# Layer 1 of a four-layer image network: column hats placed by 0/1 matmuls in three groups of rows, and PSUM in single banks

## The chip, the core and the metric

The kernel runs on one NeuronCore of a Trainium2 chip. The metric is device time in microseconds for one execution, and the time given is the median of several runs. All arithmetic is fp32.

## The reference

The input `x` has 8 images of 384 channels and 32 x 32 pixels. Four layers follow each other, each as `x = x + layer(group_norm(x))`: layer 0 is attention over the pixels, layer 1 a deformable convolution, layer 2 attention over the channels, layer 3 a sum of depthwise convolutions. The change lies in layer 1, whose core is this:

```
c3, c5, c7 = split(x, 3, axis=1)                    # 128 channels each, K = 3, 5, 7
for each c, K:
    offsets = conv2d(c, ow, ob, pad=K//2)           # 2*K*K planes: dy, dx of every tap
    acc = 0
    for each tap k = (ky, kx):
        py = y - pad + ky + dy_k;  px = x - pad + kx + dx_k
        acc += bilinear(c, py, px) * w[c, k]        # zero outside of the image
    out = conv1x1(acc, pw, pb)
out = concat(out3, out5, out7)
out = out * sigmoid(fc2(relu(fc1(mean(out)))) + fc2(relu(fc1(max(out)))))
```

A bilinear sample weighs a pixel by a product of two hats, `relu(1 - |py - row|)` and `relu(1 - |px - column|)`. So a sample is a sum over the pixels of a patch, weighted by a row hat times a column hat.

## The kernel before, in words

Layers 0, 2 and 3 stand before and after layer 1 and are, but for one statement in layer 0, not touched. Layer 1 (`layer1`) runs over 8 images and, for each, over the three kernel sizes ("cells", `CELLS`: r = 0, 1, 2 for K = 3, 5, 7).

**Cells, strips, tasks.** The output positions are cut into cells of `th x tw` pixels; all samples of a cell lie in a patch of `wy x wx` pixels: 8 x 16 = 128 for K = 3 and 5, 12 x 10 = 120 for K = 7. A strip is a column of cells (K = 3, 5: four strips, nine pixels wide) or three columns (K = 7: seven strips, six wide, the last with only two taps across). A task is one strip with a group of tap rows: ky 0 to 2 for K = 3; 0 to 2 and 3 to 4 for K = 5; 0 to 3 and 4 to 6 for K = 7. An image has 4 + 8 + 14 = 26 tasks.

**What one task needs.** 
- The patch's pixels, transposed so that pixels lie on partitions: `xw`, loaded by `patches` from DRAM images (L631), four transfers on GpSimd's queue for each column of cells.
- The sample weights: a tile of `weights` (two of them, in turn), pixel on the partition and (tap, position) along the row. `sample_weights` loads the row hats into it (`s<-hat`, L655: four transfers, each row hat repeated over the columns), loads the column hats of two tap rows each into a `plane` (`pl<-hat`, also L655, four transfers each, two buffers, each column hat repeated over the rows), and multiplies the one by the other on VectorE, one instruction for each tap row (L675).
- `sample` then multiplies the patches by the weights on TensorE (L704), two patches into a pair of PSUM banks, two such pairs in turn, and ScalarE copies a pair to SBUF (L712, tile `z`).
- `accumulate` adds `z` times the tap's weight to the accumulator on VectorE (L738), one instruction for each tap.

**Where the hats come from.** `offsets` normalizes the image (L213), transposes it and writes the DRAM images (`im<-xT`, L510), convolves the offsets on TensorE (L530; weights `cw` loaded on SyncE's queue, L523, for up to four taps, two buffers), adds positions and writes them to DRAM (`pos<-off`, L551). `hats` reads them back (`d<-pos`, L569, on SyncE's queue), makes hats on ScalarE (L583, L594) and writes them to DRAM (`hat<-hs`, L611, on ScalarE's queue).

**Order.** Layer 1 is under a manual schedule: every engine's instructions stand in the order in which the program emits them. The main loop goes over tasks. In turn i it issues the loads of task i + 1 (row and column hats) and part of the next strip's patches. Then it goes over slots, two patches each: one slot of task i's samples, a share of task i - 1's accumulations, and steps of the two background stages `offsets` and `hats`, which are paced by `LEADS` (0.75 and 0.6 of an image ahead) in equal steps per slot. If `hats` comes to a unit whose offsets aren't finished, `advance` runs the rest of those offsets at once. After the slots come the products (L675) of task i + 1. `end` projects a finished K (TensorE, L221 by the helper `project`), and after the third K the gate, as a "tail", is spread over the next slots (`or<-od` loads, L791; L792).

In layer 0, `zeros` is set and `clear` writes zeros to the DRAM images and to parts of the hats (L161, L170, GpSimd's queue) before the first image is loaded.

Of the kernel before, what the change touches and what calls it, by code (L numbers as in the profile page):

```python
# [40 lines left out]
class Cells:  # L41
# [8 lines left out]
    def __init__(self, ks, th, tw, nc, up, down, left, right, groups):  # L50
# [18 lines left out]
        if self.wx == 16:  # L69
            self.blocks = [(0, 0, 0, 0), (64, 8, 0, 0), (32, 0, 4, 0), (96, 8, 4, 0)]  # L70
            self.rows, self.lines = self.wy, list(range(self.wx))
        else:
            self.blocks = [(0, 0, 0, 0), (64, 0, 4, 0), (32, 0, 8, 0), (96, 8, 0, 4)]

            self.rows, self.lines = 32, [0, 1, 2, 3, 4, 5, 6, 7, 8, 8, 8, 9, 9, 9, 9, 9]
# [23 lines left out]
PLANE = 2 * max(c.ks * c.sp for c in CELLS)  # L99
# [25 lines left out]
def kernel(ctx: ExitStack, tc: tile.TileContext, t, out):  # L125
# [21 lines left out]
    for r, g in enumerate(CELLS):  # L147
        for i in range(2):
            images[r, i] = dpool.tile([g.cols, g.wy, g.ny, P], F32, tag=f"im{r}{i}", name=f"im{r}{i}")
            for a, n in enumerate((g.rows, len(g.lines))):  # L150
# [119 lines left out]
    def layer0():  # L270
        with tc.tile_pool(name="l0w", bufs=1) as wp, tc.tile_pool(name="l0", bufs=1) as sp, tc.tile_pool(
# [17 lines left out]
            nc.vector.memset(zeros, 0.0)  # L289
            clear(zeros)  # L290
# [114 lines left out]
            for i in range(len(todo) + 1):  # L405
                ahead = todo[i] if i < len(todo) else None
# [28 lines left out]
    def layer1(x2):  # L435
        with tc.tile_pool(name="l1w", bufs=1) as wp, tc.tile_pool(name="l1", bufs=2) as sp, tc.tile_pool(
            name="l1v", bufs=1, space=PSUM
        ) as pv, tc.tile_pool(name="l1m", bufs=2, space=PSUM) as pm, tc.manual_schedule():
# [22 lines left out]
            for i in range(2):  # L461
                h = wp.tile([P, max(g.pitch for g in CELLS) * H], F32, tag=f"hs{i}", name=f"hs{i}")
                nc.vector.memset(h, 0.0)
                hs.append(h)
            weights, sums = [], []
            for i in range(2):
# [3 lines left out]
                v = pv.tile([P, 2, HALF], F32, tag=f"v{i}", name=f"v{i}")  # L470
                nc.vector.memset(v, 0.0)
                sums.append(v)
            state = {}
            turn = [0]

            def offsets(b, r):
# [13 lines left out]
                for n0 in range(0, -(-N // px), QCH):  # L490
                    chunks = range(n0, min(n0 + QCH, -(-N // px)))
                    pt = pm.tile([P, QCH, P], F32, tag="m", name=f"pt_{b}_{r}_{n0}")
# [3 lines left out]
                    xT = sp.tile([P, QCH, P], F32, tag="tmp", name=f"xT_{b}_{r}_{n0}")  # L496
# [18 lines left out]
                po = pm.tile([P, N], F32, tag="m", name=f"po1_{b}_{r}")  # L515
                for ky in range(ks):
                    for kx in range(ks):
                        k = kx % WCH
                        if k == 0:
                            m = min(WCH, ks - kx)  # L520
                            cw = sp.tile([P, WCH * CELLS[-1].pm], F32, tag="cw", name=f"cw_{b}_{r}_{ky}_{kx}")
                            cw = cw[:, : m * g.pm].rearrange("p (k o) -> p k o", k=m)
                            nc.sync.dma_start(cw, t[f"ow{r}"][:, ky, kx : kx + m])  # L523
                        y, x = PAD - ks // 2 + ky, PAD - ks // 2 + kx
                        rows = H // g.pieces
                        for i in range(g.pieces):
                            for h in range(max(1, g.pn // HALF)):
                                n = min(g.pn, HALF) // W
                                y0 = y + i * rows + h * n
                                mm(  # L530
                                    po[i * g.pm : (i + 1) * g.pm, h * HALF : h * HALF + n * W],
                                    lhsT=cw[:, k, :],
                                    rhs=xp[:, y0 : y0 + n, x : x + W],
# [3 lines left out]
                        yield  # L537
                m = g.pieces * g.pm
                off = sp.tile([P, N], F32, tag="off", name=f"off_{b}_{r}", bufs=1)
                place = sp.tile([P, N], F32, tag="tmp", name=f"place_{b}_{r}")  # L540
                nc.sync.dma_start(place[:m, : g.pn], t[f"place{r}"])
                nc.scalar.activation(off[:m, : g.pn], po[:m, : g.pn], AF.Identity, bias=om[r])  # L542
# [11 lines left out]
            def hats(b, r):  # L554
# [9 lines left out]
                def load(kx, part):  # L564
                    d = sp.tile([P, N], F32, tag="d", name=f"d_{b}_{r}_{kx}_{part[0]}", bufs=1)
                    at = 0
                    for a in part:
                        w = (g.wy, len(g.lines))[a]
# [11 lines left out]
                for j, (kx, part) in enumerate(todo):  # L580
# [22 lines left out]
                    for a in part:  # L603
                        w = (g.wy, len(g.lines))[a]
# [35 lines left out]

            def sample_weights(i, b, r, s, k0, k1):

                g = CELLS[r]
                lo, nk = g.taps(s)
                tap = nk * g.sp
                wt = weights[i % 2]

                def spread(dst, a, ky, m):

                    tiles = hatsof[r, a, b % 2]  # L650
                    hat = tiles[0][s] if nk == g.ks else tiles[1][0]
                    src = hat[0, ky, 0, :]
                    row = g.ks * tap
                    for p0, x0, y0, more in g.blocks:
                        nc.gpsimd.dma_start(  # L655
                            dst[p0 : p0 + 32, : m * tap],
                            bass.AP(
                                tensor=src.tensor,
                                offset=src.offset + (x0 if a else y0) * row,
                                ap=[[row if a else more * row, 8], [0 if a else row, 4], [1, m * tap]],  # L660
                            ),
                        )

                pairs = [(ky, min(2, k1 + 1 - ky)) for ky in range(k0, k1 + 1, 2)]
                planes = []
                for ky, m in pairs:
                    pl = sp.tile([P, PLANE], F32, tag="plane", name=f"pl_{i}_{ky}")
                    spread(pl, 1, ky, m)
                    planes.append(pl)
                spread(wt[:, SGAP:], 0, k0, k1 + 1 - k0)  # L670
                yield
                for j, (ky, m) in enumerate(pairs):
                    for y in range(m):
                        dst = wt[: g.q, SGAP + (ky + y - k0) * tap :][:, :tap]
                        nc.vector.tensor_tensor(dst, dst, planes[j][: g.q, y * tap : (y + 1) * tap], ALU.mult)  # L675

            def sample(i, b, r, s, k0, k1):
# [10 lines left out]
                for p0 in range(i0, i1 + 1, 2):  # L688
                    n = min(2, i1 + 1 - p0)
                    v = sums[(p0 - i0) // 2 % 2]  # L690
                    for j in range(n):
                        y0 = (p0 + j) * g.th
                        lo, hi = max(k0, y0 - (H - 1)), min(k1, y0 + g.th - 1)
                        for x in range(s * g.nc, min((s + 1) * g.nc, g.nx)):
# [8 lines left out]
                            dst = v[:, j, : taps * g.th * g.sw].rearrange("p (k t x) -> p k t x", t=g.th, x=g.sw)  # L703
# [10 lines left out]
                        v[:, :n, : taps * g.th * g.sw].rearrange("p j (k f) -> p j k f", k=taps),  # L714
# [33 lines left out]
            def end(b, r):  # L748
                acc = state.pop(("acc", b, r)).rearrange("p h w -> p (h w)")
                po = pm.tile([P, N], F32, tag="m", name=f"pp_{b}_{r}")  # L750
                project(po, [pw[:, r, :]], [acc])
# [4 lines left out]
                nc.scalar.activation(o, po, AF.Identity, bias=pb[:, r : r + 1], accum_out=se[:, r, 0:1])  # L756
# [3 lines left out]
                yield  # L760
                nc.vector.tensor_reduce(se[:, r, 1:2], o, AX.X, ALU.max)
# [5 lines left out]
                pf = pm.tile([P, N], F32, tag="m", name=f"pf_{b}")  # L767
# [6 lines left out]
                for c in range(CT):  # L774
                    for i in range(2):
                        mm(
                            pf[:, HALF + c : HALF + c + 1],
# [7 lines left out]
                nc.scalar.activation(gate, pf[:, HALF : HALF + CT], AF.Sigmoid)  # L785
# [9 lines left out]
            def run(gen):  # L795
                for _ in gen:
                    pass
# [32 lines left out]
            def slots_of(b, r, s, k0, k1):  # L830
                return -(-((H - 1 + k1) // CELLS[r].th - k0 // CELLS[r].th + 1) // 2)
# [559 lines left out]
```

## Time and profile before

| | |
|---|---|
| median of 3 runs | 10046.43 us (10031.03 to 10050.84) |
| the profiled execution's own time | 10028.23 us |
| its span, first to last instruction | 10026.3 us |
| mean granted TensorE clock | 0.805 |
| TensorE busy | 6818.8 us (68%) |
| VectorE busy | 3773.1 us (38%) |
| ScalarE busy | 2332.4 us (23%) |
| GpSimd busy | 1798.7 us (18%) |
| moved by DMA | 1500.81 MB in 587308 packets |
| of that from GpSimd's queue (q0) | 1045.17 MB |

Every line of a group names the line of the kernel, the engine, the operation and the tiles as `out<-in`, then shape and count; in brackets is the idle time of the engine just before, with what ended it. Each fp32 matmul appears as two MATMUL and two LDWEIGHTS instructions. The busy share in forty slices has one digit for each 250 us. GpSimd's transfers show as busy time of that engine (issue); a transfer on SyncE or ScalarE as a row of SPq or ACTq.

### The profile page before, as it was taken

To read this page: it belongs to the slowest core of one execution; us is meant where nothing else is said; L and a number is where in the kernel's file an instruction comes from. 1 tells how busy PE (TensorE), PEld (TensorE's weight loads), DVE (VectorE), ACT (ScalarE), POOL (GpSimd) and SP (SyncE) were. 2 spreads that over 40 slices of the span, in tenths; PEclk is the share of its full clock that TensorE was granted. 3 is DMA by queue.
4 is the path that set the end of the run, shared out by engine and by line. 5 is a ranking of instruction groups with operands and counts; after the bars stand their busy time and mean duration, and the time that the engine had idled before them with its cause. 6 is when DMAs were issued, how large, how long until landed. Compare 5 with 4: busy or idle time off the path is not lost.

```text
span 10026.3 us, 90890 instructions
## 1 busy us (share of the span) xinstructions
PE 6818.8 (68%) x35337; PEld 4023.8 (40%) x35337; DVE 3773.1 (38%) x6046; ACT 2332.4 (23%) x3107; POOL 1798.7 (18%) x3352
## 2 busy tenths in 40 slices
PE   6899999999655556555645645645655554888854
PEld 2334444444223433443433433434334444444443
DVE  2233333333213434444444444344344455222232
ACT  1222222222213223232232132232232221111100
POOL 0000000000012322232233233233233332000001
PEclk8889999999876777767867867767777776888877
DMA  2130000000137857777688688688687686000053
GB/s 72 35 47 21 18 7 18 18 14 12 49 120 253 247 189 262 223 254 240 202 275 246 190 283 250 184 278 245 187 269 237 221 275 204 19 21 24 19 153 106
DMA packets 587308, 1500.81 MB, mean 150 GB/s; under 512 B 249124, under 2 KB 411180, under 8 KB 525972
## 3 DMA queue, kind: packets, MB, share of 16 engines
q0 software_dynamic: 291424, 1045.17, 33.4%
q1 hardware_dynamic: 154896, 312.55, 10.3%
q10 hardware_dynamic: 140548, 137.17, 4.5%
q8 instruction: 283, 4.64, 0.2%
q14 instruction: 157, 1.29, 0.0%
HBM read 1245.01 MB, written 248.48 MB: 149 GB/s over the span
## 4 chain that ended last, share of the span: by engine, by line
PE 46%; DMA 34%; DVE 6%; issue 4%; ACT 4%; POOL 3%; SPq 2%; ACTq 1%; DVEq 0%; POOLq 0%
PE po L530 9%; DMA xw<-im 8%; PE s L343 6%; DMA s<-hat 6%; PE pa L366 6%; PE s L355 5%; DMA pl<-hat 5%; PE v L704 4%; DMA cw<-in_ow_dram 3%; PE pqk L1087 3%; DVE s L675 3%; DMA hat<-hs 2%; PE po L221 2%; PE pc L1200 2%; POOL pl L655 2%
## 5 line engine op out<-in xcount | busy, mean ns | idle before, releaser
L704 PE MATMUL v<-s,xw 120*128 120x168 f32 (+6 forms) x10560 | 2108.1, 365 | 2012.3 <-DVE s L675 1048.5
L704 PEld LDWEIGHTS v<-s,xw 120*128 120x128 f32 (+1 forms) x10560 | 1881.5, 239 | 2363.1 <-issue 1696.6
L712 ACT ACTIVATE z<-v 128x1008 f32<-128x1008 f32 (+9 forms) x1536 | 988.8, 654 | 3223.9 <-PE v L704 2638.1
L738 DVE SCALAR_TENSOR_TENSOR acc<-z,dw,acc 128x192 f32<-128x192 f32 (+8 forms) x3496 | 1468.5, 425 | 669.5 <-ACT z L712 559.1
L675 DVE TENSOR_TENSOR s<-s,pl 120x1344 f32<-120x1344 f32 (+3 forms) x648 | 882.2, 1418 | 1414.8 <-DMA s<-hat 945.7
L530 PE MATMUL po<-xp,cw 128*98 128x512 f32 (+2 forms) x2944 | 1014.9, 617 | 525.5 <-DMA cw<-in_ow_dram 525.5
L655 POOL DMA_DIRECT2D pl<-hat x1408 | 752.1, 553 | 2443.7 <-DVE s L675 2263.9
L345 DVE TENSOR_REDUCE mx<-s 128x1 f32<-128x1024 f32 x512 | 604.5, 1219 | 1292.3 <-PE s L343 1292.2
L631 POOL DMA_DIRECT2D xw<-im x864 | 462.3, 547 | 2685.7 <-DMA im<-xT 1973.6
L358 ACT ACTIVATE e<-s 128x1024 f32<-128x1024 f32 x512 | 498.2, 1021 | 1480.6 <-PE s L355 1480.5
L530 PEld LDWEIGHTS po<-xp,cw 128*98 128x98 f32 (+2 forms) x2944 | 325.9, 156 | 1061.1 <-issue 891.4
L355 PE MATMUL s<-q,k 49*128 49x512 f32 x2048 | 651.4, 648 | 93.5 <-DVE mx L345 68.8
L343 PE MATMUL s<-k,q 49*128 49x512 f32 x2048 | 650.8, 669 | 5.4 <-ACT e L358 2.5
L366 PE MATMUL pa<-e,va 128*49 128x512 f32 x2048 | 615.5, 634 | 3.2 <-ACT e L358 3.2
L655 POOL DMA_DIRECT2D s<-hat x768 | 409.8, 547 | 703.8 <-PE v L704 481.2
L343 PEld LDWEIGHTS s<-k,q 49*128 49x128 f32 x2048 | 369.8, 316 | 277.3 <-issue 189.3
L355 PEld LDWEIGHTS s<-q,k 49*128 49x128 f32 x2048 | 267.4, 195 | 453.8 <-issue 263.7
L544 DVE TENSOR_REDUCE viol<-off 128x1 f32<-128x256 f32 (+2 forms) x24 | 18.6, 776 | 959.9 <-ACT off L542 959.9
L1200 PE MATMUL pc<-xT,hk 32*32 32x232 f32 (+6 forms) x9984 | 242.1, 436 | 174.1 <-issue 90.9
L1216 POOL DMA_DIRECT2D xr<-x x96 | 51.1, 550 | 1483.6 <-DVE gs L206 1082.2
L1087 PE MATMUL pqk<-wqk,xn 128*128 128x384 f32 x768 | 270.3, 517 | 9.5 <-DVE xn L213 9.5
L1200 PEld LDWEIGHTS pc<-xT,hk 32*32 32x32 f32 x9984 | 179.6, 114 | 236.2 <-issue 146.1
(141 smaller groups left out, 4309.4 us busy)
## 6 DMA issues: line engine op xcount, KB each, us to landing
pl<-hat POOLq DMA_DIRECT2D x576, 336.0 KB, 6.6
s<-hat POOLq DMA_DIRECT2D x192, 672.0 KB, 12.7
xw<-im POOLq DMA_DIRECT2D x608, 208.0 KB, 12.2
s<-hat POOLq DMA_DIRECT2D x192, 504.0 KB, 8.2
pl<-hat POOLq DMA_DIRECT2D x256, 360.0 KB, 6.5
s<-hat POOLq DMA_DIRECT2D x128, 540.0 KB, 8.9
s<-hat POOLq DMA_DIRECT2D x128, 360.0 KB, 7.6
hat<-hs ACTq DMA_DIRECT2D x112, 378.0 KB
```

What stands on the lines that cost most here:

```text
L343: mm(ps[j][:, hs], lhsT=q[rows, n:N:QCH], rhs=k[rows, hs], start=True, stop=True)
L345: nc.vector.tensor_reduce(mx[:, j, n : n + 1], ps[j], AX.X, ALU.max, negate=True)
L355: mm(ps[j][:, hs], lhsT=k[rows, n * P : (n + 1) * P], rhs=q[rows, hs], start=True, stop=True)
L366: mm(pa[rows, halves[h]], lhsT=va[:, n, 2 * g + j, :], rhs=state["e", n % 2, j][:, halves[h]], start=(n == 0), stop=(n == QCH - 1),)
L530: mm(po[i * g.pm : (i + 1) * g.pm, h * HALF : h * HALF + n * W], lhsT=cw[:, k, :], rhs=xp[:, y0 : y0 + n, x : x + W], start=(ky == 0 and k ...
L655: nc.gpsimd.dma_start(dst[p0 : p0 + 32, : m * tap], bass.AP(tensor=src.tensor, offset=src.offset + (x0 if a else y0) * row, ap=[[row if a ...
L675: nc.vector.tensor_tensor(dst, dst, planes[j][: g.q, y * tap : (y + 1) * tap], ALU.mult)
L704: mm(dst[:, (lo - k0) * nk : (hi + 1 - k0) * nk, :, xl * g.tw : (xl + 1) * g.tw], lhsT=state["xw", b, r, s][: g.q, xl, p0 + j, :], rhs=rhs ...
L712: nc.scalar.activation(z[:, :, yy : yy + n * g.th, :].rearrange("p k (j t) x -> p j k (t x)", j=n), v[:, :n, : taps * g.th * g.sw].rearran ...
L738: nc.vector.scalar_tensor_tensor(dst, z[:, (ky - k0) * nk + kx - first, ky - i0 * g.th : ky - i0 * g.th + H, bx : bx + x1_ + 1 - x0], dw[: ...
L1087: mm(pq[:, i, :C], lhsT=xn[:, c, n * P : (n + 1) * P], rhs=wqk[:, c, i * C : (i + 1) * C], start=(c == 0), stop=(c == CT - 1),)
L1200: mm(ps[32 * j : 32 * j + 32, i, lo * B : hi * B], lhsT=hk[32 * i : 32 * i + 32, j, (RL - d) * PITCH : (RL - d) * PITCH + W], rhs=xT[32 * ...
```

## The change

The column hats are no longer repeated by DMA. `load_columns` loads each of the patch's `wx` columns once, for two (K = 3, 5) or three (K = 7) tap rows at a time, into a tile `hx`: the row is cut into three parts (`PARTS`), which lie at partitions 0, 32 and 64. These loads are on SyncE's queue, three for each `hx`, five buffers, and stand two tasks ahead. For each tap row, three matmuls with a matrix of zeros and ones (`sel`) put the columns on the patch's pixels, each part into one of three PSUM banks (`columns`, one buffer), and VectorE multiplies the row hats by that PSUM tile. The products of task i + 1 stand in the second half of task i's slots.

PSUM is laid out anew: three single banks for the samples instead of two pairs, with as many patches in a bank as fit (`together`), one bank for transposes, projections and the gate, one for the offset convolution, three for `columns`. So the K = 7 convolution does one half of the image after the other, and loads its weights twice (four `cw` buffers); the projection does its halves one by one. The steps that pace the background are counted for the new loops. The hats of K = 7 are made for ten columns and not for sixteen lines. In layer 0 the clearing of the DRAM images stands at the fifth pair of heads of the main loop.

```diff
+        self.column = [0] * P
+        for p0, x0, _, more in self.blocks:
+            for p in range(32):
+                self.column[p0 + p] = x0 + (p // 12 if more else p // 4)
+        self.deep = 32 // self.wx
...
+PARTS = 3
+PART = max(c.ks * c.sp for c in CELLS) // PARTS
+SEL = [(w, m, j) for w in sorted({c.wx for c in CELLS}) for m in range(1, 32 // w + 1) for j in range(m)]
...
-            nc.vector.memset(zeros, 0.0)
-            clear(zeros)
...
             for i in range(len(todo) + 1):
+                if i == PAIRS:
+                    tc.keep_in_program_order(nc.vector.memset(zeros, 0.0))
+                    clear(zeros)
...
+            sel = wp.tile([P, len(SEL), P], F32, tag="sel", name="sel")
+            nc.scalar.dma_start(sel, t["sel"])
...
-                v = pv.tile([P, 2, HALF], F32, tag=f"v{i}", name=f"v{i}")
+            for i in range(3):
+                v = pv.tile([P, HALF], F32, tag=f"v{i}", name=f"v{i}")
...
+            columns = pv.tile([P, PARTS, HALF], F32, tag="columns", name="columns")
...
-                po = pm.tile([P, N], F32, tag="m", name=f"po1_{b}_{r}")
-                for ky in range(ks):
-                    for kx in range(ks):
...
+                for h in range(max(1, g.pn // HALF)):
+                    n = min(g.pn, HALF)
+                    po = pm.tile([P, HALF], F32, tag="c", name=f"po1_{b}_{r}_{h}")
+                    for ky in range(ks):
+                        for kx in range(ks):
...
-            def sample_weights(i, b, r, s, k0, k1):
+            def load_columns(i, b, r, s, k0, k1):
...
+                for ky in range(k0, k1 + 1, g.deep):
+                    m = min(g.deep, k1 + 1 - ky)
+                    hx = sp.tile([P, PART], F32, tag="hx", name=f"hx_{i}_{ky}", bufs=5)
                     src = hat[0, ky, 0, :]
-                    for p0, x0, y0, more in g.blocks:
-                        nc.gpsimd.dma_start(
-                            dst[p0 : p0 + 32, : m * tap],
...
+                    for c in range(PARTS):
+                        nc.sync.dma_start(
+                            hx[32 * c : 32 * c + m * g.wx, :n],
                             bass.AP(
...
+                                tensor=src.tensor, offset=src.offset + c * n, ap=[[g.ks * tap, g.wx], [tap, m], [1, n]]
                             ),
                         )
+                    state["columns", i] += [(hx, m, j) for j in range(m)]
...
-                for j, (ky, m) in enumerate(pairs):
-                    for y in range(m):
-                        dst = wt[: g.q, SGAP + (ky + y - k0) * tap :][:, :tap]
-                        nc.vector.tensor_tensor(dst, dst, planes[j][: g.q, y * tap : (y + 1) * tap], ALU.mult)
+                for ky, (hx, m, j) in enumerate(state.pop(("columns", i))):
+                    k = SEL.index((g.wx, m, j))
+                    for c in range(PARTS):
+                        rows = slice(32 * c, 32 * c + m * g.wx)
+                        mm(columns[: g.q, c, :n], lhsT=sel[rows, k, : g.q], rhs=hx[rows, :n], start=True, stop=True)
+                    dst = wt[: g.q, SGAP + ky * tap :][:, :tap].rearrange("p (c n) -> p c n", c=PARTS)
+                    nc.vector.tensor_tensor(dst, dst, columns[: g.q, :, :n], ALU.mult)
+                    yield
+
+            def together(r, s, k0, k1):
+                g = CELLS[r]
+                return HALF // ((k1 - k0 + 1) * g.taps(s)[1] * g.th * g.sw)
...
-                for p0 in range(i0, i1 + 1, 2):
-                    n = min(2, i1 + 1 - p0)
-                    v = sums[(p0 - i0) // 2 % 2]
+                few = together(r, s, k0, k1)
+                for p0 in range(i0, i1 + 1, few):
+                    n = min(few, i1 + 1 - p0)
+                    v = sums[turn[1] % len(sums)][:, : n * taps * g.th * g.sw].rearrange("p (j f) -> p j f", j=n)
+                    turn[1] += 1
...
-                po = pm.tile([P, N], F32, tag="m", name=f"pp_{b}_{r}")
-                project(po, [pw[:, r, :]], [acc])
...
+                for h in range(2):
+                    hs_ = slice(h * HALF, (h + 1) * HALF)
+                    po = pm.tile([P, HALF], F32, tag="m", name=f"pp_{b}_{r}_{h}")
+                    mm(po, lhsT=pw[:, r, :], rhs=acc[:, hs_], start=True, stop=True)
+                    nc.scalar.activation(o[:, hs_], po, AF.Identity, bias=pb[:, r : r + 1], accum_out=half[:, h : h + 1])
...
-                sum(g.ks**2 + 6 + -(-H // g.th // QCH) for g in CELLS),
+                sum(g.ks**2 * max(1, g.pn // HALF) + 6 + -(-H // g.th // 4) for g in CELLS),
...
                 if i + 1 < len(tasks):
-                    need(1, tasks[i + 1][:2])
                     nxt = sample_weights(i + 1, *tasks[i + 1])
                     next(nxt)
+                    n = tasks[i + 1][4] - tasks[i + 1][3] + 1
+                    products = [slots // 2 + (slots - slots // 2) * k // n for k in range(n)]
+                    if i + 2 < len(tasks):
+                        need(1, tasks[i + 2][:2])
+                        load_columns(i + 2, *tasks[i + 2])
...
-                        while nadd < total * (j + 1) / (slots - 1):
+                        while nadd < total * (j + 1) / slots:
...
+                    for _ in range(products.count(j)):
+                        next(nxt)
...
+    sel = np.zeros((P, len(SEL), P), np.float32)
+    for k, (wx, m, j) in enumerate(SEL):
+        column = next(c.column for c in CELLS if c.wx == wx)
+        for i in range(PARTS):
+            for x in range(wx):
+                sel[32 * i + x * m + j, k] = np.array(column) == x
```

## The prediction

> **What bounds the kernel now.** I read the page first: the span, then the 40 slices.
>
> ```profile
> span 10026.3 us, 90890 instructions
> ...
> PE   6899999999655556555645645645655554888854
> ...
> DVE  2233333333213434444444444344344455222232
> ...
> PEclk8889999999876777767867867767777776888877
> DMA  2130000000137857777688688688687686000053
> ```
>
> Three stages show. In the ends (layers 0, 2 and 3) TensorE is full and the DMA engines are idle. Between 2700 and 8500 us (layer 1, where the change lies) no engine is full: TensorE about 0.55, VectorE 0.4, DMA 0.75. So layer 1 is bound by waits, and I need them by region. One image takes 704 to 708 us there; the view of busy time by stretches, cut at one image's borders (3x3 cells; 5x5 cells; 7x7 cells; a block of offset convolution inside the 7x7 cells; their rest), gives:
>
> ```profile
> core 0: us, PE busy (x) PEld busy (x) DVE busy (x) ACT busy (x) POOL busy (x), PEclk, DMA share, GB/s
> 5092.00:5188.00 96.00, 35.44 (x159) 30.31 (x159) 34.25 (x54) 30.35 (x55) 34.14 (x64) 0.66 0.87 292
> 5188.00:5404.00 216.00, 128.56 (x531) 78.77 (x532) 89.78 (x135) 65.45 (x109) 63.76 (x120) 0.75 0.78 257
> 5404.00:5619.00 215.00, 109.37 (x619) 96.19 (x619) 119.86 (x220) 58.98 (x72) 76.60 (x144) 0.73 0.87 265
> 5619.00:5692.00 73.00, 73.00 (x168) 27.24 (x167) 0.00 (x0) 1.05 (x1) 0.00 (x0) 1.00 0.18 46
> 5692.00:5800.00 108.00, 50.37 (x295) 48.52 (x294) 66.19 (x136) 33.46 (x45) 42.24 (x80) 0.67 0.72 220
> ```
>
> TensorE works 397 of 708 us and VectorE 310; where the convolution does not run alone, DMA is near 0.9. The timeline of one 7x7 task shows why (columns: start, us, engine, line):
>
> ```profile
> 5462.94 4.27 POOL L655 DMA_DIRECT2D pl<-hat  x8 [12.03 <-DVE s L675]
> 5467.49 0.54 POOL L655 DMA_DIRECT2D s<-hat  x1 [0.28 <-PE v L704]
> ...
> 5470.98 1.04 POOL L655 DMA_DIRECT2D s<-hat  x2 [1.94 <-DMA pl<-hat]
> ...
> 5491.66 5.96 DVE L675 TENSOR_TENSOR s<-s,pl 120x1344 f32<-120x1344 f32 x4 [15.19 <-DMA xw<-im]
> ...
> 5496.26 1.19 PE L704 MATMUL v<-s,xw 120*128 120x126 f32 x4 [23.46 <-DVE s L675]
> ```
>
> The column hats (pl) can load only when VectorE has freed the planes, the row hats (s) queue behind them on GpSimd, the four products come 20 us later, and TensorE waits 23.5 us. A strip (two tasks) takes 55 us here (product at 5436.28, next at 5491.66). This wait for data, not an engine, sets layer 1; "DMA xw<-im" in the brackets is just the transfer seen last. The chain of waits over the image agrees, and names the other large piece, the convolution L530:
>
> ```profile
> by line: PE po L530 15.3%; DMA s<-hat 13.8%; DMA xw<-im 12.6%; DMA pl<-hat 7.9%; PE v L704 7.1%; DMA cw<-in_ow_dram 5.6%; issue 4.7%; DVE s L675 4.3%; DMA im<-xT 3.4%; POOL pl L655 3.3%; DMA or<-od 3.1%; DVE acc L738 1.7%; SPq L510 1.7%; DM
> ```
>
> **Two rules of the Trainium skill.** "TensorE: Matmul & The Clock Gate", Part 3 (Packing small matmuls), says that matmuls whose contraction fits 32 rows run at the same time when their operands start at different partitions 32i, and gives 3.07x for four. The nearest trace row has two groups of rows, at 0 and 64:
>
> ```profile
> 1002.06 2.11 PE L343 MATMUL s<-k,q 49*128 49x512 f32 x8
> ```
>
> Alone, an instruction of 512 columns takes 0.437 us (168 in 73.48 us, the block above), so eight would take 3.5: a gain of 1.66, not 2. It fits if each fp32 matmul is two instructions, the two of one matmul follow each other, and the next matmul starts with the second: five steps of 0.437 = 2.18. I go by the trace. "DMA: Bandwidth & Descriptors", section "Issuing engines are not separate DMA queues", says all queues share the same 16 engines, so moving loads from GpSimd to SyncE buys only issue time. The trace agrees as far as it goes (DMA share 0.75 over the image with three queues), so I count bytes, not queues.
>
> **Step 1, what leaves.** By the DMA issues of one image, pl is 192 transfers and 50.3 MB of 167.6. The new hx loads carry each row once, not 8 or 12 times: 20.0 MB / 8 + 30.3 MB / 12 = 5 MB. Left: 122 MB. GpSimd loses 192 x 0.55 = 106 us of issue; more to the point, s no longer stands behind 4.3 us of pl issue and 2.7 MB of pl data. At 290 GB/s (DMA nearly full above) s lands 9 us (2.0 MB) or 12 us (2.7 MB) after issue, 2 us of latency included; now it takes 20 to 28 from the first pl. SyncE gains 123 issues of about 0.35 us (43 us); it queues them ahead of its cw and d loads, but they are for two tasks on, with five buffers, so I cost them at nothing. If that cover fails, cw comes later still.
>
> **Step 2, what TensorE gains.** 81 products an image (12, 20, 42 and 7, of 3 x 288, 480, 448 and 128 columns). At 0.854 ns a column one pass is 0.25, 0.41, 0.38 and 0.11 us. By the pattern above three groups take 4 passes, plus 0.2 for changing the array's shape (the first L343 took 820 ns, the others 589): 1.2, 1.8, 1.7, 0.65 us, in all 14 + 36 + 71 + 5 = 126 us an image. Bounds: 2 passes, 56 us; in turn, 6 passes and the change of shape, 184 us.
>
> **Step 3, VectorE.** Same 648 products; one operand is now in PSUM. No such row exists; L395 (PSUM) takes 1283 ns and L792 (SBUF) 1285 for the same shape, so nothing is added. They no longer come as one burst at the task's end, but are spread over the second half, and TensorE waits for each before the next, since there is one `columns` buffer.
>
> **Step 4, the path by region**, TensorE's order with the waits that I expect.
> - 7x7 strip: samples 12.1 + 10.1, products 7 x 1.7 = 12, waiting for the last product at two task starts 2, for s in the second task 5 (products can start after seven slots, 8 us, and s needs 12): 41 us against 55. VectorE's 49 x 0.424 + 7 x 1.55 = 31.6 fits under it. Six strips 246; short strip 24 (now 30).
> - Convolution: its pace counts steps, and halving each 7x7 step makes 161 steps an image for 107. Counting the loop through, the block in the 7x7 cells falls from 42 steps x 4 instructions (73.5 us) to 64 x 2 (56 us); 30 steps (26 us) and 13 of 5x5 (8 us) are spread over the strips, 12 us of that inside waits for s; its cw loads stall about 13 x 1.5 = 20. 7x7 in all: 246 + 24 + 56 + 34 - 12 + 20 = 368, now 396.
> - 5x5: per strip samples 17, products 5 x 1.8 = 9, waits 6: 32 x 4 = 128; convolution 10, cw stalls 10, projection and hats on ScalarE 8: 156, now 216 (cw alone stalled it some 50).
> - 3x3: samples 4, products 3.6, waits 5: 12.6 x 4 = 50, and the tail's od/or transfers, unchanged, 26: 76, now 96.
>
> 600 us an image for 708. First and last image have other shares of convolution, so I count 7 images, not 8: -750 us. Single PSUM banks: 87 more evacuations an image x 0.155 us of fixed cost (from 1008 columns in 1.051 and 756 in 0.827) = 13 us of ScalarE, hidden under TensorE; the projection's second half waits for the first to be read, 24 x 1 = 24 us, within the 8 above. If ScalarE's hats hold up the three buffers, that cover is gone, at about 2 us each for 22 hats an image.
>
> **Step 5, layer 0.** The clearing of the images starts at pair 4, not at 10 us. It now delays kflat (20 us) and three or four divisions (den, inv, bc: 53, 41, 23, 20 us). Later it meets the same divisions of other pairs; only the start is won. I take -20, between -40 and +40.
>
> Sum against the profiled execution (10028.2 us, span 10026.3): 10028 - 750 - 20 = 9258. The profiled execution lies 18 us below the median of the three runs (10046.43): 9276, rounded **9280**.
>
> **Rivals.**
> - *Row groups in turn.* Step 2 at its upper bound: +58 an image. For it: L343's 1.66 instead of 2. 600 + 58 = 658, times 7: 9280 + 406 = about 9690.
> - *TensorE fits better.* Step 2 at 56 us and s early enough for no wait: 600 - 70 = 530, 9280 - 490 = 8790. For it: the clock, 0.75 now, rises with denser work (1.00 in the block).
> - *Turn-taking, slower.* One `columns` buffer, and both engines in order: each of 81 products keeps TensorE until VectorE has drained what is ahead, product 1.55 plus two slots' accumulations (4 x 0.42) = 3.2 us, 260 an image, of which I counted about 80. 780 an image, 7 x 72 = +500 on the time before: 10,550. It decides from 1.3 us a product (108 / 81) beyond mine. Against: VectorE is busy only 310 of 708.
> - *No change.* Row groups in turn and s as late as now (13 us landing plus issue, 2 to 5 more a task): about 10,030.
>
> **Numbers.** Forecast 0.52, in turn 0.18, better 0.13, slower 0.14, no change 0.03. A measurement of this kernel tells 0.2% from no change. Faster 0.83, same 0.03, slower 0.14. The range, 8650 to 9950, holds the first three with their bounds and leaves out 0.17.
>
> **What would show it.** Right: pl and its 50 MB gone, DMA share about 0.6; product matmuls in threes of about 1.5 us; six 7x7 strips near 41 us; convolution blocks of 128 instructions, 56 us; an image near 600. Wrong: product groups of 2.3 us (in turn); TensorE waiting on VectorE's product two or three us each time (turn-taking); s landing at 13 us or later; cw stalls grown because SyncE stands at an hx load.

## The result, and the profile after

The changed kernel takes 10,156.76 us (median of 6 runs, 10,141.92 to 10,180.61) beside 10,050.42 us for the kernel before in the same session: a ratio of 1.0104, interval 1.0082 to 1.0127. It is 1.0% slower. The forecast was 9,280.

The page of the profile after, the span and the slices (one digit for each 250 us):

```profile
span 10161.1 us, 99025 instructions
...
PE   8887999999755676676776766766766776788854
...
DMA  1113000000145555655565565566566565000053
```

What was to leave has left: in layer 1 the DMA share falls from 7 or 8 tenths to 5 or 6, and TensorE's digits rise from about 5 to 6 or 7. And yet nothing is won. Two marks in the traces say where the time is. They are the first patch load of layer 1 and the first matmul of layer 2, before and then after (duration in ns, minimum/median/maximum; first and last start in us):

```profile
L631 POOL DMA_DIRECT2D xw<-im x864: 508/546/737, 2708.1 to 8424.0; - x173
L1087 PE MATMUL pqk<-wqk,xn x768: 486/486/1008, 8522.3 to 9450.0; 128*128 128x384 f32 x192
```

```profile
L646 POOL DMA_DIRECT2D xw<-im x864: 506/567/987, 2782.3 to 8557.2; - x173
L1140 PE MATMUL pqk<-wqk,xn x768: 486/486/980, 8664.8 to 9587.6; 128*128 128x384 f32 x192
```

Layer 1 starts 74 us later, so layer 0 lost 74. It takes 5,882 us for 5,814 and loses 68. The rest gained 8.

One image of layer 1, busy time by stretches (3x3; 5x5; 7x7; the block of convolution inside the 7x7 cells). The border between 5x5 and 7x7 is the first 7x7 sample here; the prediction's lay some 28 us later, so I compare those two as a sum.

```profile
5199.00:5275.00 76.00, 46.59 (x230) 33.98 (x230) 34.19 (x53) 21.63 (x37) 17.98 (x35) 0.70 0.76 256
5275.00:5486.00 211.00, 127.70 (x551) 72.80 (x548) 86.78 (x131) 69.76 (x143) 28.74 (x56) 0.77 0.56 173
5486.00:5916.00 430.00, 310.76 (x1472) 191.42 (x1470) 185.71 (x358) 113.27 (x200) 65.56 (x124) 0.82 0.57 153
5762.00:5819.00 57.00, 56.22 (x131) 21.05 (x130) 1.89 (x2) 1.34 (x3) 0.00 (x0) 1.00 0.24 61
```

The 3x3 cells take the 76 us that were forecast, and the block 56 to 57. The other two take 641 us where 524 were forecast. TensorE is busy 485 of 717 us (395 of 706 before); 232 us are waits. The waits of TensorE over this image, before and then after (columns: who waited for whom, us, times, the longest):

```profile
PE po L530 <- DMA cw<-in_ow_dram: 68.0, 7, 21.0
```

```profile
PE po L547 <- DMA cw<-in_ow_dram: 96.8, 8, 18.4
PE columns L705 <- DVE s L707: 78.3, 24, 19.6
PE v L744 <- ACT z L752: 19.2, 8, 7.2
```

The largest is not in the sampling at all: the offset convolution waits for its weights, eight times, 12 us each. The timeline of one such wait:

```profile
5641.91 1.07 PE L547 MATMUL po<-xp,cw 128*98 128x512 f32 x2
5642.36 2.12 POOL L694 DMA_DIRECT2D s<-hat  x4 [19.74 <-PE v L744]
...
5644.45 2.16 POOL L646 DMA_DIRECT2D xw<-im  x4
...
5649.40 1.30 SPq L584 DMA_DIRECT2D d<-pos  x2
...
5650.74 1.06 SPq L543 DMA_DIRECT2D cw<-in_ow_dram  x2
...
5666.47 2.02 PE L547 MATMUL po<-xp,cw 128*98 128x512 f32 x2 [18.38 <-DMA cw<-in_ow_dram]
```

The weights are issued at the point of the program where they are used, behind whatever SyncE did just before. Row hats and patches are on the way then, and TensorE goes on 15.7 us after the weights' issue. It does nothing else in these 18 us: the samples and products that stand behind the convolution in its order wait too.

The same timelines of all these waits of the image, each cut at the moment in which the load is issued, divide the time. After, 39 of the 97 us pass before the issue, 32 of them in three waits in which SyncE still issues `im<-xT` writes, and 58 between issue and landing. Before, it was 37 and 31 of 68. So the part that grew is the landing.

### The profile page after: what moved, and what is told of

Read it like the earlier page. It is cut to its first block, busy times and chain, and to the rows that moved or that the text cites. A ratio compares the mean times of both kernels' runs of the same rounds, so it can differ in the third digit from the quotient of the medians.

```text
span 10161.1 us, 99025 instructions
## 1 busy us (share of the span) xinstructions
PE 7578.5 (75%) x39225; PEld 4166.3 (41%) x39225; DVE 3761.8 (37%) x6071; ACT 2454.4 (24%) x3899; POOL 976.3 (10%) x1816
## 4 chain that ended last, share of the span: by engine, by line
PE 54%; DMA 25%; DVE 8%; ACT 4%; SPq 3%; issue 3%; POOL 1%; ACTq 1%; DVEq 0%; POOLq 0%
DMA s<-hat 9%; PE po L547 8%; PE v L744 8%; PE s L351 6%; PE pa L374 6%; PE s L363 5%; PE columns L705 5%; DMA cw<-in_ow_dram 4%; DVE s L707 3%; PE pqk L1140 3%; PE po L231 2%; SPq L525 2%; PE pc L1253 2%; PE pq L231 2%; DMA im<-xT 2%
## 5 line engine op out<-in xcount | busy, mean ns | idle before, releaser
L744 PE MATMUL v<-s,xw 120*128 120x168 f32 (+6 forms) x10560 | 2144.1, 357 | 291.2 <-ACT z L752 210.9
L744 PEld LDWEIGHTS v<-s,xw 120*128 120x128 f32 (+1 forms) x10560 | 1824.7, 230 | 1093.4 <-ACT z L752 532.2
L752 ACT ACTIVATE z<-v 128x378 f32<-128x378 f32 (+6 forms) x2232 | 1093.3, 504 | 3176.4 <-PE v L744 2879.8
L707 DVE TENSOR_TENSOR s<-s,columns 120x1344 f32<-120x1344 f32 (+3 forms) x648 | 918.8, 1418 | 2232.7 <-PE columns L705 1453.1
L547 PE MATMUL po<-xp,cw 128*98 128x512 f32 (+2 forms) x2944 | 1071.8, 615 | 705.7 <-DMA cw<-in_ow_dram 699.4
L705 PE MATMUL columns<-hx,sel 30*120 30x448 f32 (+4 forms) x3888 | 763.7, 666 | 692.7 <-DVE s L707 661.1
L705 PEld LDWEIGHTS columns<-hx,sel 30*120 30x120 f32 (+3 forms) x3888 | 238.2, 219 | 847.3 <-DVE s L707 724.0
L1253 PE MATMUL pc<-xT,hk 32*32 32x224 f32 (+6 forms) x9984 | 238.8, 427 | 183.2 <-issue 104.0
L374 PEld LDWEIGHTS pa<-e,va 128*49 128x49 f32 x2048 | 104.3, 126 | 402.8 <-issue 342.3
## 6 DMA issues: line engine op xcount, KB each, us to landing
s<-hat POOLq DMA_DIRECT2D x192, 672.0 KB, 10.5
```

The source lines that it names most:

```text
L374: mm(pa[rows, halves[h]], lhsT=va[:, n, 2 * g + j, :], rhs=state["e", n % 2, j][:, halves[h]], start=(n == 0), stop=(n == QCH - 1),)
L547: mm(po[i * g.pm : (i + 1) * g.pm, :n], lhsT=cw[:, k, :], rhs=xp[:, y0 : y0 + n // W, x : x + W], start=(ky == 0 and kx == 0), stop=(ky == ...
L705: mm(columns[: g.q, c, :n], lhsT=sel[rows, k, : g.q], rhs=hx[rows, :n], start=True, stop=True)
L707: nc.vector.tensor_tensor(dst, dst, columns[: g.q, :, :n], ALU.mult)
L744: mm(dst[:, (lo - k0) * nk : (hi + 1 - k0) * nk, :, xl * g.tw : (xl + 1) * g.tw], lhsT=state["xw", b, r, s][: g.q, xl, p0 + j, :], rhs=rhs ...
L752: nc.scalar.activation(z[:, :, yy : yy + n * g.th, :].rearrange("p k (j t) x -> p j k (t x)", j=n), v.rearrange("p j (k f) -> p j k f", k= ...
```

## The experiments

Ratios are to the kernel before, from runs of the same session; us are medians. The kernel before took 10,046 to 10,061 us in these sessions, so a difference of two medians from different sessions can be off by some 15 us.

| run | edit | us | ratio, interval |
|---|---|---|---|
| e1 | zero fill first | 10,104.2 | 1.0065, 1.0047 to 1.0083 |
| e2 | convolution weights two chunks ahead | 9,735.7 | 0.9706, 0.9686 to 0.9727 |
| e3 | kernel before, weights one chunk ahead | 9,834.1 | 0.9800, 0.9777 to 0.9823 |
| e4 | products last | 10,543.3 | 1.0497, 1.0478 to 1.0515 |
| e5 | e2, row hats in two parts | 9,341.6 | 0.9302, 0.9283 to 0.9320 |
| e6 | e2, transposed image in blocks of eight | 9,609.0 | 0.9568, 0.9552 to 0.9584 |
| e7 | e2, no placing | 9,364.3 | 0.9318, 0.9302 to 0.9333 |
| e8 | hx issued by GpSimd | 10,090.0 | 1.0044, 1.0028 to 1.0060 |
| e9 | row hats in two parts | 9,836.2 | 0.9777, 0.9751 to 0.9804 |
| c1 | e1, e2, e5 and e6 | 9,179.3 | 0.9129, 0.9103 to 0.9155 |
| c2 | kernel before, weights one ahead, row hats in two | 9,643.9 | 0.9590, 0.9564 to 0.9615 |
| c3 | c1, hx issued by GpSimd | 9,156.4 | 0.9100, 0.9065 to 0.9134 |

**e1, zero fill first.**

```diff
             zeros = sp.tile([64, 1, max(g.ny * P for g in CELLS)], F32, tag="zeros", name="zeros")
+            nc.vector.memset(zeros, 0.0)
+            clear(zeros)
...
-                if i == PAIRS:
-                    tc.keep_in_program_order(nc.vector.memset(zeros, 0.0))
-                    clear(zeros)
```

> The changed kernel with the zeros written to the DRAM images at the very start of layer 0 again, as before; all else stays. Theory (layer 0 loses 74 us because the zero fill now runs beside the divisions, layer 1 loses the other 68): 10,157 - 74 = about 10,085 us, and the patches of layer 1 start near 2,708 us again instead of 2,782. Rival (the place of the zero fill costs nothing by itself, layer 0's 74 us come from something else that the change moved): within 20 us of 10,157.

It gave 10,104, about 53 us less (39 by the ratios), and in its trace layer 1 starts at 2,712.6. So the place of the fill is the cause of layer 0's loss; the timed gain is a little under the trace's 70. The traces show the mechanism. Busy time from 750 to 1000 us, after and then in e1:

```profile
750.00:1000.00 250.00, 194.33 (x553) 78.75 (x552) 61.69 (x79) 42.46 (x43) 11.54 (x15) 0.81 0.28 46
```

```profile
750.00:1000.00 250.00, 246.45 (x801) 109.00 (x802) 84.62 (x103) 65.34 (x66) 0.00 (x0) 0.99 0.12 23
```

TensorE is full in this stretch when no fill runs (GpSimd's busy time, the fifth pair of numbers, is that of its issues). And the chain of waits in the same stretch of the changed kernel holds the tiny transfers of the attention's division, one of them (4 KB; start, us):

```profile
816.06 33.93 DMA den<-att
```

In the first 1,250 us the division's three transfers (den, inv, bc) make up 8.9, 5.1 and 6.4% of the chain (255 us), against 6.1, 4.2 and 4.0% (179 us) before. The last projection of the first image starts 74 us earlier with the late fill (460 for 534 us before), that of the second image 15 later, of the third 60 and of the fourth 72.

The fill doesn't load the DMA engines evenly. The zeros for the hats (L180) come in two bursts of small packets: between 797 and 850 us, 9,480 of 9,882 packets are under 512 bytes. From 800 to 840 us the mean share of the DMA engines is 0.90 and then 0.65 (20 us each), from 980 to 1,020 us 0.72 and 0.67, and yet only 43 to 60 GB/s move. Each burst meets a division of the chain: the `den` transfer above, and one of `bc` of 29.1 us at 988. Just before and between the bursts such transfers take 5.5 to 8 us, so the two hits explain some 48 of the 76 us. Before, the bursts stand at 540 to 600 and 740 to 760 us, and in e1 close to that; there the chain has no division.

**e2, weights ahead.** The first two chunks are loaded at the head of `offsets`, each further one at the use of the chunk two before it (`load_cw(n)` makes the tile and loads chunk n).

```diff
...
+                for n in range(2):
+                    load_cw(n)
                 xs = sp.tile([P, N], F32, tag="tmp", name=f"xs1_{b}_{r}")
...
-                                nc.sync.dma_start(cw, t[f"ow{r}"][:, ky, kx : kx + size])
+                                cw = loaded[chunks_cw.index((h, ky, kx))]
+                                load_cw(len(loaded))
```

> The changed kernel with the weights of the offset convolution loaded two chunks ahead on SyncE's queue (the first two ahead of the image's own load); number of loads, bytes and buffers as in the changed kernel. Theory (TensorE's 97 us an image of waits for these weights is what ate the gain of layer 1): most of 8 x 97 us comes back, 9,450 to 9,700, about 9,600, and the waits of the convolution on the cw transfer fall from 700 us to under 150. Rival turn-taking (the one columns buffer makes TensorE wait for VectorE, and that sets the pace): the waits for cw turn into waits for VectorE's product, 10,000 or more. Rival SyncE's queue blocked by the hx loads: cw is as late as before however early it stands, 10,100 to 10,160.

It gave 9,736: 421 us less, a little short of the theory's 450 to 700. The waits of one image of 671 us:

```profile
PE columns L717 <- DVE s L719: 83.4, 27, 20.4
PE v L756 <- ACT z L764: 35.6, 13, 6.1
PE po L559 <- DMA cw<-in_ow_dram: 12.7, 1, 12.7
```

The wait for weights falls by 84 us, the image by 46: nearly half of the stalled time had been cover for others, whose waits now show (at `z` 36 us for 19, at the normalized image `xs` 28 for 15). Over the layer the wait for weights is 106 us for 699. Neither rival holds: the turn-taking wait grows by 5 us only, and the weights come in time with the hx loads in the same queue.

**e3, the kernel before with weights ahead.** The same edit with one chunk and two buffers.

> The kernel before with its convolution weights loaded one chunk ahead on SyncE's queue (two buffers as before, no room for more). Theory (a load that stands at its use is exposed in either kernel, 68 us an image before): 8 x 68 = 540 us at most, and as one chunk ahead is shorter than the landing beside the planes' transfers, about half: 9,700 to 9,900, about 9,800. Rival (before, the column hats' transfers set the pace and the stalls of cw are hidden behind them): 10,000 to 10,050.

9,834, as expected: the flaw is older than the change.

**e4, products last.**

```diff
-                    products = [slots // 2 + (slots - slots // 2) * k // n for k in range(n)]
+                    products = []
```

> The changed kernel with all products of a task after its last slot, as they stood before, instead of spread over the second half of the slots. Theory (the waits at the products, 78 us an image, are mostly row hats that have not landed, and turn-taking costs little as long as other work lies between products): the row hats are then there, but TensorE stands still for each of VectorE's 1.4 us products, 81 x 1.4 = 113 us an image for 78: 10,157 + 8 x 35 = about 10,440. Rival turn-taking (each spread product keeps TensorE until VectorE has drained accumulations queued ahead, so a burst at the end is cheaper): 9,900 to 10,100.

10,543, slower as the theory said. In a burst every product makes TensorE wait for VectorE; spread out, samples fill that time. The spread is right.

**e5, row hats in two parts.** The first products need only the first tap rows.

```diff
+                part = (k1 + 2 - k0) // 2 * tap
+                for at, n_ in ((0, part), (part, size - part)):
                     for p0, x0, y0, more in g.blocks:
                         nc.gpsimd.dma_start(
-                            wt[p0 : p0 + 32, SGAP : SGAP + size],
+                            wt[p0 : p0 + 32, SGAP + at : SGAP + at + n_],
```

> The changed kernel with the convolution weights two chunks ahead, and the row hats of each task loaded in two parts (eight transfers for four; first half of the tap rows first), same bytes. Against the run with the weights ahead alone (9,736 us, in which TensorE still waits 88 us an image at the products). Theory (these waits are mostly row hats that have not landed; the first products need only the first half): 25 to 45 us an image back, 9,380 to 9,540, about 9,460. Rival turn-taking (they come from the one columns buffer and VectorE's queue): 9,700 to 9,760.

9,342: 394 us less than e2, more than the theory's 200 to 360. Turn-taking as the cause of most of these waits is out. The waits at the products in one image of 616 us:

```profile
PE columns L719 <- DVE s L721: 47.7, 22, 20.6
```

By the DMA issues the median landing falls from 10.4 us (672 KB) to 7.5 (336 KB), and that of the patches queued behind from 13.7 to 8.9. The waits at the products fall by 36 of the 54 us by which the image is shorter; another 12 are TensorE's own busy time (476 us for 488, at a granted clock of 0.83 for 0.81). What remains at the products includes one wait of 20.6 us for VectorE, which itself stands for the gate's transfers (`or<-od`), so turn-taking proper is at most 27 us an image. e9, below, shows that the repair helps without e2 as well.

**e6, transposed image in blocks of eight.**

```diff
-                    xT = sp.tile([P, 4, P], F32, tag="xT", name=f"xT_{b}_{r}_{n0}")
+                    if n0 % 8 == 0:
+                        xT = sp.tile([P, 8, P], F32, tag="xT", name=f"xT_{b}_{r}_{n0}")
+                        first = n0
...
+                    if n0 == first and n0 + 4 < -(-N // px):
+                        yield
+                        continue
```

> The changed kernel with the weights two chunks ahead, and the transposed image written to DRAM in blocks of eight chunks again (37 transfers an image for 81; each block still goes through one PSUM bank in two halves; three cw buffers for four, for room). Against 9,736. Theory (SyncE stands some 26 us at these transfers in every unit, and the loads queued behind come late): 10 to 20 us an image, 9,580 to 9,660. Rival (with the weights ahead nothing critical is queued behind them any more): 9,700 to 9,760.

9,609: 127 us less than e2, as expected. Single PSUM banks had cost more than evacuations: a block of four chunks doubled the number of `im<-xT` transfers, and SyncE stands 26 us at the 36 of one 7x7 image. The run doesn't tell which of the loads queued behind them gains.

**e7, no placing** (what it leaves out stands in its expectation).

```diff
-                    for c in range(PARTS):
-                        rows = slice(32 * c, 32 * c + m * g.wx)
-                        mm(columns[: g.q, c, :n], lhsT=sel[rows, k, : g.q], rhs=hx[rows, :n], start=True, stop=True)
```

> The changed kernel with the weights two chunks ahead, without the matmuls that place the column hats: VectorE multiplies the row hats by a PSUM tile of ones, so the column hats are left out of the result; their loads stay. It prices the placing as a whole. Theory (TensorE's own 90 us an image for the placing, less what then shows as waiting for row hats): 50 to 80 us an image, 9,100 to 9,340, about 9,250. Rival turn-taking (with the matmuls all 88 us of waiting for VectorE go too): under 8,700. Rival (TensorE's work is hidden in waits for data): 9,600 to 9,740.

9,364, 24 us above the theory's upper end: the whole placing costs 372 us, 46 an image. TensorE's own time for it is 95 us an image (763.7 us in all by the groups), so half of it lies in time that would be waiting anyway.

**e8, hx issued by GpSimd.** In `load_columns`, `nc.sync.dma_start` becomes `nc.gpsimd.dma_start`.

> The changed kernel with the column hats' loads (hx) issued by GpSimd and not by SyncE; convolution weights at their use as in the change. Theory (cw waits grew from 68 to 97 us an image because the weights are loaded in 41 pieces for 27, not because of hx in SyncE's queue): within 60 us of 10,157. Rival (SyncE stands at hx loads, and cw behind them): the waits fall by 29 us an image, about 9,930.

10,090: 67 us less (60 by the ratios), just past the theory's 60 and far from the rival's 230. Between 2,800 and 8,200 us TensorE still waits 661.6 us for weights, beside 689.5. So SyncE standing at hx loads is a small part of it.

**e9, row hats in two parts only.**

> The changed kernel with the row hats in two parts only; convolution weights at their use as in the change. If the waits for weights and for row hats don't overlap: 10,157 - 394 = about 9,760. Theory (they overlap in part: while TensorE stands for weights, row hats land): 9,800 to 9,900. Rival (waits for weights take all of it): 10,050 or more.

9,836: within the theory's range. The repair is worth 321 us here and 394 once the weights come early: the two waits overlap in part.

**c2, the kernel before with both repairs.** As e3, and the row hats' `spread` in two calls.

> The kernel before with convolution weights one chunk ahead and the row hats in two parts. It asks what the change itself is worth once both kernels are mended. Theory (before, the row hats stand behind 2.7 MB of planes on GpSimd's queue, so that half of them lands hardly earlier): 9,780 to 9,840, against 9,834 with the weights alone. Rival (the row hats' landing is what matters in both kernels): 9,500 to 9,600.

9,644: 190 us less than e3, between theory and rival. My reason, that half of the row hats would hardly land earlier behind the planes, falls: their median landing goes from 13.3 to 8.6 us. It also says what the change is worth when both kernels are mended alike: 9,342 (e5) for 9,644, 302 us (289 by the ratios), with the late zero fill still in it.

**c1, all four repairs.** Three `cw` buffers, for room.

> The changed kernel with all four: zero fill first, convolution weights two chunks ahead, row hats in two parts, transposed image in blocks of eight. If the four costs lie in different places of the image, the single gains add: 9,342 - 127 - 53 = about 9,160 (9,120 to 9,240). If they cover each other (one wait ends where the next would have), 9,280 to 9,340.

9,179, as if the four add. One image, by stretches as above, and its waits for weights and at the products:

```profile
4757.00:4833.00 76.00, 45.78 (x236) 33.04 (x230) 34.16 (x53) 21.54 (x37) 27.54 (x53) 0.70 0.77 250
4833.00:5005.00 172.00, 127.35 (x549) 71.90 (x546) 86.93 (x131) 68.66 (x142) 45.71 (x87) 0.81 0.73 215
5005.00:5357.00 352.00, 307.30 (x1475) 193.30 (x1475) 185.50 (x359) 113.53 (x201) 95.64 (x181) 0.87 0.69 188
```

```profile
PE columns L723 <- DVE s L725: 44.1, 20, 21.7
PE po L563 <- DMA cw<-in_ow_dram: 3.5, 1, 3.5
```

The same work in 600 us for 717: TensorE's busy time is nearly that of the changed kernel (480 for 485); its waits fall from 232 to 120 us.

**c3, and hx on GpSimd.**

> The four repairs together and the column hats' loads issued by GpSimd. Theory (with the weights ahead, SyncE's queue holds nothing that is urgent but the image's own load x, whose lateness makes TensorE wait 20 to 25 us an image at the transposes; GpSimd's queue has room): 0 to 60 us under the four repairs alone. Rival (hx in GpSimd's queue stands ahead of the row hats and delays them): 20 to 100 us over it.

9,156; the intervals of c1 and c3 overlap, so they are not told apart. Both beat both kernels: 8.7% and 9.0% under the kernel before.

## Why the prediction was wrong

The sum missed by 877 us: 94 in step 5 (+74 for -20), 818 in step 4 (+68 for -750), less 35 in the rest (the other layers gained 8, and the profiled run of the changed kernel is not below its median). Point by point:

- **Step 1 (bytes): right.** 122 MB an image, as forecast, and pl is gone. Row hats of 672 and 504 KB land in 10.5 and 8.1 us (12 and 9). The hx loads cost little (e8).
- **Step 2 (products): too dear, on the safe side.** A group of 448 columns takes 1.02 us when TensorE comes to it without a long wait, 1.20 in the mean; 1.7 was forecast. 95 us an image for 126. *Row groups in turn* (2.3 us) is refuted.
- **Step 3 (VectorE): right.** The product with a PSUM operand takes 1418 ns in the mean, for 648 products as before.
- **Step 4 (the path): failed in the term "cw stalls".** I put 13 x 1.5 = 20 us in the 7x7 cells and 10 in the 5x5; measured are 58 and 39, together 97 for 30. The number to use stood in the trace of before: seven waits, 68 us, 9.7 each. I saw these stalls, named them in the chain (5.6%) and put "some 50" on them in the 5x5 cells, and then priced them at 1.5 us each and gave no reason. But such a wait is the landing of the load and whatever SyncE still issues ahead of it, and neither shrinks with the work that follows. It grew, from 9.7 to 12.1 us.
- **Other terms of step 4.** The waits for ScalarE's `z` and `xT` and for VectorE's normalized image `xs` were 8 us for "projection and hats"; measured are 42, and 35 stood in the trace of before. With cw this makes 101 of the 117 us by which the image is too long. TensorE's own time was wrong in two places that nearly cancel: the convolution takes 137 us an image where the sum has 56 + 26 + 8 + 10 = 100 (127 before), the products about 95 for 126. The remaining 10 to 15 us I haven't assigned. The 3x3 cells met their 76 us in part by luck: their samples take 31 us for 16 (32 before), and the tail, 26 in the sum, shows as one wait of 19.6 us. The waits for row hats and the last product were about as forecast; what I had not seen is that they could be halved (e5).
- **Single PSUM banks: not hidden.** The evacuations were; the doubled `im<-xT` transfers weren't (e6, 127 us).
- **Step 5 (zero fill): wrong sign.** "Only the start is won" was right, and came to 74 us at the first image. "It meets the same divisions" was wrong: the later images lost 148. The prediction treats the fill as an even load. It has two bursts; at the new place both meet a division, and at the old place, by luck of the order, neither did (e1). No run shifts the bursts alone.
- **The slower rival, turn-taking,** had the right side and the wrong cause. The waits at the products halve when the row hats come in pieces, so most of them were never turn-taking. The last sentence of the prediction had the true sign, grown stalls at cw, with a reason, hx, that is a small part at most (e8). Why each stall grew is not settled. The doubled `im<-xT` transfers are not it by the image shown: the time before the issue stayed at 37 to 39 us, and the landing grew from 31 to 58. No run separates what made the landing longer.

So the design gives about what was forecast, 600 us an image, only when the weights' load, the row hats' load and the `im<-xT` writes around it are mended (c1); that the sum agrees is partly chance, since its terms differ.

## What to carry to other kernels

A load that stands at its use in an in-order queue costs its landing time and what the queue still holds ahead of it, whatever the size of the work behind it: take the mean wait from the trace, times the number of waits, and load ahead before anything else is tuned. When a consumer takes a tile piece by piece, load it in those pieces and in that order. A background transfer that is moved isn't gone: look for its bursts and price them against what runs at its new place.

## What I had not expected of the hardware

- **A long wait costs twice.** In the timeline of the changed kernel above, two convolution instructions take 1.07 us at 5641.91 and 2.02 us at 5666.47, after the wait of 18.4 us. Product groups of 448 columns take 1.02 us, and 1.86 in this image after waits of 3.6 us and more, for example:

```profile
5566.38 1.02 PE L705 MATMUL columns<-hx,sel 30*120 30x448 f32 x6 [0.78 <-DVE s L707]
5845.90 1.86 PE L705 MATMUL columns<-hx,sel 30*120 30x448 f32 x6 [9.94 <-DVE s L707]
```

  The Trainium skill, "TensorE: Matmul & The Clock Gate", Part 1, says that the array falls to half its clock after about 3.4 us of idling; these rows agree with it. Over one image the granted clock is 0.79 after and 0.83 in c1.
- **A fill of small packets keeps the DMA engines busy while it moves little.** While `den<-att`, 4 KB, took 33.9 us, the mean share of the DMA engines was 0.71 up to 834 us and 0.42 up to 850, at 53 and 38 GB/s. In the 3x3 cells of the changed kernel a share of 0.76 moved 256 GB/s. The mean over 250 us, 0.28 (the stretch shown under e1), hides this.
- **Three row groups overlap better than two had.** Three groups of 448 columns take 1.02 us, where the prediction's pass for one instruction of 448 columns is 0.38: 2.7 passes for six instructions. Two groups of 512 took 4.8 passes for eight (2.11 us at 0.437).
